# Compact bfloat16 images, borders filled once, and loop constants through DRAM in a fused convolution, state-space and expert kernel

## The chip, the cores and the metric

The kernel runs on one core of one Trainium2 chip. The metric is device time in microseconds. Its median before the change is 2576.19 us over three runs (2576.03 to 2581.16).

## The reference, cut

The input `x` has 128 images of 128 channels and 16 x 16 pixels. Layer 0 is a quantised convolution block; layer 1 treats each image as 256 tokens of 128 channels.

```python
h = _act_quant(_bn(gn(x), gamma1, beta1))        # 4 bits: round(clip(v, 0, 1) * 15) / 15
out = _conv3x3(h, _weight_quant(w1) * pat1)      # pat1: a cross, 5 of 9 taps
out = _act_quant(_bn(out, gamma2, beta2))
out = _conv3x3(out, _weight_quant(w2) * pat2)    # pat2: the diagonals, 5 of 9 taps
x = x + out + gn(x)
t = to_tokens(x)
t = t + mamba(ln(t)) + reverse(mamba(reverse(ln(t))))   # chunks of 64, 4 heads, state 64
t = t + experts(ln(t))                                  # softmax router, best 2 of 8
x = from_tokens(t)
```

`_bn` uses the mean and the variance of the whole batch, so nothing of the first convolution can start before all of `x` has been read, and nothing of the second before the first is done.

## The kernel before

**Loading.** Two images at a time make a tile `xr[i]` of 128 channels x 512 floats (256 KB). There are 64 of them, loaded by SP's queue (L377), and they stay in SBUF through both convolutions. Statistics of each tile run on DVE and ACT as it lands, and become one scale and one bias per image and channel (`sc1`, `bi1`), which hold the group norm, the batch norm and the factor 15 together.

**The two convolutions.** `by_weights` picks one of two programs on a value that the device works out from the weights; here it is the one with five taps and one bfloat16 weight part (`nq` is 1). In the first (`conv1`, from L493), `quantised(i)` brings a tile to the range of the levels: one of its two images by ACT with a Relu (L502), the other mostly by POOL with a scale and a bias (L504) and a second pass that takes the maximum with zero (L506; on DVE for every third tile). `quantise` then writes the levels into one of four padded images `hpads` of 2 x 18 x 18. Before the change these are float32: DVE takes the minimum with 15 and adds the constant `HALF` (L195), which rounds to a whole number n and leaves a float whose lower half is, read as bfloat16, the number 128 + n. `low(hp)` reads only these lower halves, at a step of 4 bytes. `pads` writes the border of all four images on POOL, at the start of each convolution. `conv3x3` (L218) does five matmuls of 128 x 128 weights on 512 pixels, and `offsets` works out what the added 128 contributes, as a constant `less` per channel. ACT takes the result to `o1` (L519), DVE takes its statistics (L520), and SP's queue stores it to DRAM (L522), but for the first five tiles, which are kept (`NKEPT`).

The second (`conv2`, from L546) fetches the `o1` tiles (L558), runs ACT's Relu (L562) and the same `quantise`, convolves, scales the residual `xr` on POOL (L592) or ACT (L590), and adds on DVE (L593). `stored(i)` transposes the sum to tokens (four transposes on PE, L571), scales it on ACT (L573) and stores it to `y_d` (L574). Matmuls of both convolutions have one line, L222, and one name, `cv`.

**The loop.** It works on 64 tiles of 512 tokens. Each part of the work (`part_a` the layer norm and its transposition, `part_c` the step sizes and decays, and so on) is a generator, and a table `T` of hand-written due times per pair of tiles (`PERIOD` 375) gives the order in which their steps are issued; `manual_schedule` keeps that order. `part_a` begins with the load of `yt` from `y_d` (L712), the layer norm (L688 to L706), the transposition `u_ps` (L718) and its copy `uT` (L721). `part_c` begins with the matmul `dt_ps` (L734, L742) and `dtr` on DVE (L748).

Ahead of the loop, `constants` fills three copies of `rows` and `cols` (4 KB of bfloat16 per partition each), which hold the constant part of the segment sums' operands: by ACT (L623), DVE (L624, L628), and POOL, which selects the causal triangle (L635). POOL also zeroes `gts`, `daz` and `lwz` (L646). These tiles take the space of the convolutions, which is released before.

Of the kernel before, what the change touches and what calls it, by code (L numbers as in the profile page):

```python
# [8 lines left out]
F32 = mybir.dt.float32  # L9
BF16 = mybir.dt.bfloat16  # L10
AF = mybir.ActivationFunctionType
ALU = mybir.AluOpType
AX = mybir.AxisListType

P = 128
NT = 256
EPS = 1e-5
MAGIC = 12582912.0
HALF = MAGIC + 0x4300
OFFSET = 128.0  # L20
SCALE = 225.0
NLEV = 15.0
NH = 4
HD = 64
# [3 lines left out]
BIG = 1e38  # L28
LNMIN = 2.0 ** -60
G = 4  # L30
NKEPT = 5


@with_exitstack
def kernel(ctx: ExitStack, tc: tile.TileContext, a: dict):

    nc = tc.nc
    x_d, out_d = a["x"], a["out"]
    B = x_d.shape[0]
    NP = B // 2  # L40
# [16 lines left out]
    cum_d = [dram.tile([G * NH * 4, P], F32, name=f"cum_{i}", tag=f"cum_{i}") for i in range(2)]  # L57


    ident = const.tile([P, P], F32, name="ident")  # L60
    make_identity(nc, ident)
    magic = const.tile([P, 1], F32, name="magic")
    nc.gpsimd.memset(magic, -MAGIC)
    ones = const.tile([P, P], F32, name="ones")
    nc.gpsimd.memset(ones, 1.0)

# [116 lines left out]
        nc.gpsimd.tensor_tensor(w, t, parts[:, :, 1, :], ALU.subtract)  # L183
        nc.scalar.copy(parts[:, :, 2, :], w)

    def low(hp):

        return hp.bitcast(BF16).rearrange("p b h (w two) -> p b h w two", two=2)[:, :, :, :, 0]

    def quantise(q, hp, nq):  # L190

        at = hp[:, :, 1:17, 1:17]
        q4 = q.rearrange("p b (h w) -> p b h w", w=16)
        if nq == 1:
            nc.vector.tensor_scalar(at, q4, NLEV, HALF, ALU.min, ALU.add)  # L195
        else:
            nc.vector.tensor_scalar(q, q, NLEV, MAGIC, ALU.min, ALU.add)
            nc.vector.tensor_scalar(low(hp)[:, :, 1:17, 1:17], q4, MAGIC, None, ALU.subtract)

    def pads(nq):  # L200

        for t in hpads:
            for at in (t[:, :, 0:18:17, :], t[:, :, :, 0:18:17]):
                nc.gpsimd.memset(at, HALF if nq == 1 else 0.0)

    def offsets(pool, psums, wq, taps, nq):

# [10 lines left out]
    def conv3x3(ps, hp, wq, taps, nq):  # L218
        passes = [(tap, q) for tap in taps for q in range(nq)]
        for n, (tap, q) in enumerate(passes):  # L220
            dy, dx = tap // 3, tap % 3
            nc.tensor.matmul(  # L222
                ps, wq[:, tap, q, :], low(hp)[:, :, dy : dy + 16, dx : dx + 16],
                start=(n == 0), stop=(n == len(passes) - 1),
            )

# [34 lines left out]

    ress = ExitStack()
    res = ress.enter_context(tc.tile_pool(name="res", bufs=1))
    wq2 = res.tile([P, 9, 3, P], BF16, name="wq2")

    hpads = [res.tile([P, 2, 18, 18], F32, name=f"hpad{k}") for k in range(4)]
    for t in hpads:
        nc.gpsimd.memset(t, 0.0)
    off = res.tile([P, 2], BF16, name="off")
    nc.gpsimd.memset(off, OFFSET)  # L270
    onec = res.tile([P, P], F32, name="onec")
# [76 lines left out]
    with tc.tile_pool(name="w1p", bufs=1) as w1p:  # L348
# [15 lines left out]
        with tc.tile_pool(name="setup1", bufs=1) as setup, tc.tile_pool(  # L364
# [6 lines left out]
                next(weights)  # L371


            xr = []
            for i in range(NP):
                t = res.tile([P, 2, NT], F32, name=f"xr{i}", tag=f"xr{i}")
                nc.sync.dma_start(t, x_c[:, 2 * i : 2 * i + 2, :])  # L377
                xr.append(t)
            load_weights()
            w2 = w1p.tile([P, 9, P], F32, name="w2", tag="w")  # L380
            nc.sync.dma_start(w2, a["L0_conv_w2"])
# [109 lines left out]
        def conv1(taps, nq):  # L491
            with tc.tile_pool(name="pb", bufs=3) as pb, tc.tile_pool(
                name="psb", bufs=4, space=PSUM  # L493
            ) as psb:
                weights = conv_weights(wq2, how2, w1p, psb, w2, pat2, DIAGONAL, "c2")

                def quantised(i):
                    q = pb.tile([P, 2, NT], F32, name=f"q1_{i}", tag="q", bufs=4)
                    for k in range(2):
                        sc, bi = sc1[:, 2 * i + k : 2 * i + k + 1], bi1[:, 2 * i + k : 2 * i + k + 1]  # L500
                        if k == 0 or i % 10 == 5:
                            nc.scalar.activation(q[:, k, :], xr[i][:, k, :], AF.Relu, bias=bi, scale=sc)  # L502
                        else:
                            nc.gpsimd.tensor_scalar(q[:, k, :], xr[i][:, k, :], sc, bi, ALU.mult, ALU.add)  # L504
                            eng = nc.vector if i % 3 == 0 else nc.gpsimd
                            eng.tensor_scalar(q[:, k, :], q[:, k, :], 0.0, None, ALU.max)  # L506
                    quantise(q, hpads[i % 4], nq)

                pads(nq)
                less = offsets(pb, psb, wq1, taps, nq)  # L510
                for i in range(3):
                    quantised(i)
                for i in range(NP):
                    if i + 3 < NP:
                        quantised(i + 3)
                    ps = psb.tile([P, 2, NT], F32, name=f"cv1_{i}", tag="cv")
                    conv3x3(ps, hpads[i % 4], wq1, taps, nq)
                    o1 = kept[i] if i in kept else pb.tile([P, 2, NT], F32, name=f"o1_{i}", tag="o1")
                    nc.scalar.activation(o1, ps, AF.Identity, bias=less)  # L519
                    behind = nc.vector.bn_stats(o1st[:, i, :], o1.rearrange("p b s -> p (b s)"))  # L520
                    if i not in kept:
                        nc.sync.dma_start(o1_d[i], o1)  # L522
                    if i > 5 and i % 4 == 2:
                        with tc.issue_after(behind.ins):
                            next(weights, None)
                for _ in weights:
                    pass

                mv2 = pb.tile([P, 2], F32, name="mv2", bufs=1)
                nc.vector.bn_aggr(mv2, o1st)  # L530
                rs2 = pb.tile([P, 1], F32, name="rs2", bufs=1)
                nc.gpsimd.tensor_scalar(rs2, mv2[:, 1:2], 1.0 / SCALE**2, EPS, ALU.mult, ALU.add)
                nc.gpsimd.tensor_tensor(rs2, rs2, mhalf[:, 0:1], ALU.pow)
                nc.gpsimd.tensor_scalar(sc2, rs2, gam2, 1.0 / NLEV, ALU.mult, ALU.mult)
                tmp2 = pb.tile([P, 1], F32, name="tmp2", bufs=1)
                nc.gpsimd.tensor_scalar(tmp2, mv2[:, 0:1], sc2, -1.0, ALU.mult, ALU.mult)
                nc.gpsimd.tensor_scalar(bi2, bet2, NLEV, tmp2, ALU.mult, ALU.add)
# [8 lines left out]
    def conv2(taps, nq):  # L546
        with tc.tile_pool(name="pc", bufs=6) as pc, tc.tile_pool(
            name="psc", bufs=4, space=PSUM
        ) as psc, tc.tile_pool(name="psw", bufs=2, space=PSUM) as psw:
            pads(nq)  # L550
            less = offsets(pc, psc, wq2, taps, nq)
            weights = second_weights(pc, psw)
            qs = dict(kept)
# [5 lines left out]

            def quantised(i):  # L560
                q = qs.pop(i)
                nc.scalar.activation(q, q, AF.Relu, bias=bi2, scale=sc2)  # L562
                quantise(q, hpads[i % 4], nq)

            def stored(i):
# [39 lines left out]
    ress.close()  # L605
    kepts.close()

    late = ctx.enter_context(tc.tile_pool(name="late", bufs=1))

# [2 lines left out]
    rows = [late.tile([P, NH, 2, 2, P], BF16, name=f"rows{k}") for k in range(3)]  # L614

    cols = [late.tile([P, 2, 2, 2, 2, P], BF16, name=f"cols{k}") for k in range(3)]
    far = late.tile([HD, 1], BF16, name="far")

    def constants():
        nc.gpsimd.memset(far, -1e30)  # L620
        for k in range(3):
            r, c = rows[k], cols[k]
            nc.scalar.copy(r.rearrange("p h d t l -> p h (d t l)"), heads.unsqueeze(2).to_broadcast([P, NH, 4 * P]))  # L623
            nc.vector.tensor_copy(  # L624
                r[0:HD].rearrange("p h d t (f l) -> p (h d t f) l", l=HD),
                ident[0:HD, 0:HD].unsqueeze(1).to_broadcast([HD, 2 * NH * 2 * 2, HD]),
            )
            nc.vector.tensor_copy(  # L628
                c.rearrange("p m d j f l -> p m (d j f l)"), triple.unsqueeze(2).to_broadcast([P, 2, 8 * P])
            )  # L630
            for d in range(2):
                for half in range(2):
                    sign = 1 - 2 * d
                    for m in range(2):
                        nc.gpsimd.affine_select(  # L635
                            out=c[0:HD, m, d, :, half, :], in_=far.unsqueeze(2).to_broadcast([HD, 2, P]),
                            pattern=[[0, 2], [sign, P]], compare_op=ALU.is_ge, fill=0.0,
                            base=-sign * HD * half - 1, channel_multiplier=-sign,
                        )


    gts = [late.tile([P, P], F32, name=f"gt{k}") for k in range(2)]
    daz = late.tile([P, 2, P], F32, name="daz")
    lwz = late.tile([P, P], F32, name="lwz")
    for t in (*gts, daz, lwz):
        nc.gpsimd.memset(t, 0.0)  # L646
    pr = ctx.enter_context(tc.tile_pool(name="pr", bufs=2))
    sm = ctx.enter_context(tc.tile_pool(name="sm", bufs=2))
    ps_ = ctx.enter_context(tc.tile_pool(name="ps", bufs=1, space=PSUM))
    BANKS = {"x": 2, "y": 2, "o": 4}  # L650
    E0 = 5

# [56 lines left out]
    def part_a(i):  # L709

        yt = yts[i] = pr.tile([P, 4, P], F32, name=f"yt{i}", tag="yt", bufs=6)
        nc.sync.dma_start(yt, y_d[i])  # L712
        yield
        u = pr.tile([P, 4, P], F32, name=f"u{i}", tag="u", bufs=2)
        yield from layernorm(yt, u, f"a{i}")
# [527 lines left out]
            stream = parts[name](i // 2 if len(places) == 1 else i, *which)  # L1243
            steps += [(i // 2 * PERIOD + t, len(steps) + n, stream) for n, t in enumerate(places[i % 2])]
    steps.sort(key=lambda step: step[:2])
    constants()
    with tc.manual_schedule():
        for _, _, stream in steps:
            next(stream)


# [28 lines left out]
```

## Time and profile before

| | |
|---|---|
| median of three runs | 2576.19 us |
| the profiled execution | 2581.9 us, with a span of 2579.9 us |
| busy in the span | PE 2438.1 us (95%), DVE 2260.6 (88%), ACT 2192.9 (85%), POOL 1656.8 (64%) |
| first matmul of the first convolution | 75.28 us |
| first matmul of the second convolution | 176.19 us |
| last sum of the second convolution (L593) ends | 294.47 us |
| first transposition of the loop (`u_ps`) starts | 313.35 us |
| first `dtr` starts | 318.82 us |

The times in the table's lower half are counted from the start of the span. PE is busy in 95% of the span, but that is an average: the first 320 us, before the loop is under way, have other limits, and a change to them is to be read in them. In the lines of the profile, PE is the matmul engine, PEld its weight loads, DVE the vector engine, ACT the scalar engine, POOL the general engine, and SP the engine whose queue issues most DMA transfers. A line of a group or of the timeline names the source line, the operation, its output and inputs, the shape, how often it ran, the busy time, and in brackets or behind a bar the idle time before it and what ended it.

### The profile page before, as it was taken

What the parts mean: (1) busy time and instruction counts of PE and PEld (TensorE: products, weight loads), DVE (VectorE), ACT (ScalarE), POOL (GpSimd) and SP (SyncE); (2) the same over time, 40 slices, a digit from 0 to 9 for tenths busy, and PEclk for the clock granted to TensorE, in tenths of its full rate; (3) what the DMA queues carried; (4) which work ended last, traced back from release to release, by engine and by line L of the source; (5) the groups of instructions that cost most, each with busy time, mean ns of one, the idle gap of its engine ahead of it and who ended that gap; (6) DMA issues with size and microseconds to landing.
All of it is one profiled execution on the core that took longest, in us unless ns stands there. A gap on an engine that the chain in (4) does not pass through costs nothing.

```text
span 2579.9 us, 49413 instructions
## 1 busy us (share of the span) xinstructions
PE 2438.1 (95%) x15940; PEld 1484.6 (58%) x15940; DVE 2260.6 (88%) x6193; ACT 2192.9 (85%) x4482; POOL 1656.8 (64%) x1727
## 2 busy tenths in 40 slices
PE   0879689999999999999999999999999999999997
PEld 0235345666666666666666666666666666666663
DVE  8877589999999999999999999999999999999883
ACT  6777579998988889889888898998888898988881
POOL 1777315666667666666676666666666666666666
PEclk9989889999999999999999999999999999999998
DMA  9458423444444444444434444444444443443343
GB/s 284 147 191 286 166 62 90 123 122 120 127 122 112 130 131 125 124 124 122 121 112 125 129 129 118 120 129 121 120 120 131 131 122 119 127 125 114 108 126 104
DMA packets 303030, 339.03 MB, mean 131 GB/s; under 512 B 56865, under 2 KB 226849, under 8 KB 302753
## 3 DMA queue, kind: packets, MB, share of 16 engines
q1 hardware_dynamic: 302752, 335.68, 43.2%
q8 instruction: 132, 2.16, 0.3%
q14 instruction: 146, 1.19, 0.2%
HBM read 261.41 MB, written 57.41 MB: 124 GB/s over the span
## 4 chain that ended last, share of the span: by engine, by line
PE 88%; DVE 4%; DMA 3%; POOL 2%; ACT 2%; issue 1%; SPq 0%; POOLq 0%; DVEq 0%; ACTq 0%
PE f_ps L1157 17%; PE x_ps L845 13%; PE y_ps L980 9%; PE z_ps L888 9%; PE o_ps L1040 9%; PE sg L933 5%; PE xt_ps L900 4%; PE y_ps L986 4%; PE g_ps L919 4%; PE cv L222 3%; DMA xr<-in_x 2%; PE n_ps L1013 1%; PE u_ps L718 1%; PE u_ps L1062 1%; PE f_ps L1152 1%
## 5 line engine op out<-in xcount | busy, mean ns | idle before, releaser
L1145 POOL TENSOR_TENSOR gb<-gb,u2T 128x512 f32<-128x512 f32 x512 | 641.3, 1277 | 119.5 <-PE y_ps L986 89.9
L863 DVE SCALAR_TENSOR_TENSOR xc<-x_ps,cw,xc 128x510 f32<-128x510 f32 (+2 forms) x768 | 570.6, 743 | 47.0 <-ACT xc L857 37.2
L996 POOL TENSOR_TENSOR yg<-yg,z 128x512 f32<-128x512 f32 x256 | 325.9, 1279 | 354.5 <-DVE yg L992 155.2
L1157 PE MATMUL f_ps<-gb,ew 128*128 128x512 f32 x1024 | 511.6, 603 | 6.1 <-POOL gb L1145 5.9
L845 PE MATMUL x_ps<-uT,wx 128*128 128x512 f32 x768 | 403.6, 608 | 7.6 <-ACT e L673 3.3
L673 ACT ACTIVATE e<-sg 128x512 f32<-128x512 f32 x512 | 299.8, 592 | 49.6 <-PE sg L933 44.4
L673 ACT ACTIVATE e<-e,ends 128x128 f32<-128x128 f32 x1024 | 325.1, 392 | 0.0
L980 PE MATMUL y_ps<-e,xt 128*64 128x256 f32 x2048 | 317.7, 389 | 0.2 <-DVE yg L992 0.2
L961 DVE TENSOR_TENSOR e<-e,g_ps 128x1024 f32<-128x1024 f32 x256 | 311.2, 1216 | 5.9 <-ACT e L673 2.7
L863 DVE SCALAR_TENSOR_TENSOR bc<-x_ps,cw,bc 128x510 f32<-128x510 f32 (+2 forms) x384 | 286.3, 746 | 20.7 <-ACT bc L857 4.9
L1157 PEld LDWEIGHTS f_ps<-gb,ew 128*128 128x128 f32 x1024 | 181.2, 192 | 173.6 <-issue 137.0
L888 PE MATMUL z_ps<-uT,wz 128*128 128x512 f32 x512 | 271.2, 611 | 1.7 <-DVE xc L863 1.1
L857 ACT ACTIVATE xc<-x_ps,cb,cw 128x512 f32<-128x512 f32 x256 | 199.2, 778 | 63.6 <-PE x_ps L845 57.2
L1040 PE MATMUL o_ps<-wo,yg 128*128 128x128 f32 x2048 | 251.3, 276 | 0.2 <-DVE e L966 0.2
L1040 PEld LDWEIGHTS o_ps<-wo,yg 128*128 128x128 f32 x2048 | 240.5, 193 | 11.1 <-DVE g L1117 8.4
L992 DVE SCALAR_TENSOR_TENSOR yg<-xc,dcol,y_ps 128x512 f32<-128x512 f32 x256 | 189.3, 740 | 50.8 <-PE y_ps L986 47.2
L1028 POOL TENSOR_TENSOR rr<-rr,mhalf 128x8 f32<-128x8 f32 x64 | 110.0, 1719 | 161.5 <-DVE g L1119 82.4
L986 PE MATMUL y_ps<-e,xt 128*64 128x128 f32 x2048 | 198.9, 273 | 0.0
L933 PE MATMUL sg<-rows,cols 128*128 128x256 bf16 x1024 | 192.0, 274 | 5.8 <-ACT e L673 2.9
L222 PE MATMUL cv<-hpad,wq 128*128 128x512 bf16 x640 | 179.3, 423 | 18.8 <-DVE hpad L195 9.7
L986 PEld LDWEIGHTS y_ps<-e,xt 128*64 128x64 f32 x2048 | 146.9, 137 | 74.2 <-DVE e L966 0.5
L980 PEld LDWEIGHTS y_ps<-e,xt 128*64 128x64 f32 x2048 | 118.9, 136 | 101.0 <-issue 53.9
(257 smaller groups left out, 4873.0 us busy)
## 6 DMA issues: line engine op xcount, KB each, us to landing
gb<-gd SPq DMA_DIRECT2D x256, 512.0 KB
e<-cum SPq DMA_DIRECT2D x256, 256.0 KB
xr<-in_x SPq DMA_DIRECT2D x64, 256.0 KB
y<-yt SPq DMA_DIRECT2D x64, 256.0 KB
yt<-y SPq DMA_DIRECT2D x64, 256.0 KB
cc<-bc SPq DMA_DIRECT2D x128, 128.0 KB
out<-ob SPq DMA_DIRECT2D x64, 256.0 KB
o<-o SPq DMA_DIRECT2D x59, 256.0 KB
```

The costliest lines, as they stand in the source:

```text
L673: nc.scalar.activation(out, in_, func, **more)
L845: nc.tensor.matmul(ps, wx[d][:, n * P : (n + 1) * P], uTs[i], start=True, stop=True)
L863: nc.vector.scalar_tensor_tensor(acc[:, :, to], raw[:, :, of], cw[:, d, n, 3 - back : 4 - back], acc[:, :, to], ALU.mult, ALU.add,)
L888: nc.tensor.matmul(ps, wz[:, d, n * P : (n + 1) * P], uTs[i], start=True, stop=True)
L933: nc.tensor.matmul(sg[:, :, of], c_[:, k, d, s, half, :], r_[:, :, d, s, of], start=True, stop=True)
L961: nc.vector.tensor_tensor(e0.rearrange("p h t l -> p h (t l)"), e0.rearrange("p h t l -> p h (t l)"), gps[i, d, k][:, 0:NT].unsqueeze(1).t ...
L980: nc.tensor.matmul(y_ps[64 * q : 64 * q + 64, k, :], xt[:, 2 * k + s0, 64 * h : 64 * h + 64], e0[:, h].rearrange("p t l -> p (t l)"), star ...
L986: nc.tensor.matmul(y_ps[64 * q : 64 * q + 64, k, s1 * P : (s1 + 1) * P], xt[:, 2 * k + s1, 64 * h : 64 * h + 64], e1[:, h, :], start=False ...
L996: large(nc.gpsimd.tensor_tensor(yg, yg, zs[i, d][:, n, :], ALU.mult))
L1040: nc.tensor.matmul(o_ps[:, (2 * j + d) * P : (2 * j + d + 1) * P], ygs[i, d, n][:, t * P : (t + 1) * P], wo[d][:, n, :], start=(n == 0), s ...
L1145: large(nc.gpsimd.tensor_tensor(gb[:, e], gb[:, e], u2Ts[i], ALU.mult))
L1157: nc.tensor.matmul(f_ps, ew[:, e, :], gbs[i, e], start=False, stop=(e == NE - 1))
```

## The change

- The padded images become compact bfloat16. All of each image is filled with 128 once, early on; its number is then 128 + n with n in the low byte, so DVE writes only that byte, as uint8 at a step of two bytes, after a minimum with 15 and a maximum with 0.
- With the maximum in that instruction, the Relus become plain scale and bias and the separate maximum passes go. The share of ACT and POOL in the first convolution's scaling is set anew: ACT does 46 of the 128 images, POOL 82 (70 and 58 before).
- Six `o1` tiles are kept in place of five, and `o1` has five buffers in place of three.
- `rows` and `cols` are built once, on POOL in the load stage, and stored to DRAM (512 KB each) by POOL's queue. `constants` is six loads on SP's queue, placed in the loop's order after an early step. DVE, in place of POOL, zeroes `gts`, `daz` and `lwz`.
- The pools of the loop are opened with `reuse_waits="tile"`: a tile in released space waits for the earlier tiles that it overlaps, and not for the whole of the earlier pool. The loads of the first two `yt` tiles go to POOL's queue, and the first two steps of `part_a` are issued ahead of all others.

The order of the loop's instructions on each engine is otherwise the same. On SP's queue the six loads of constants stand behind the last store of `y` and ahead of the third `yt` load. On DVE the four fills and the statistics of the first three `yt` tiles stand ahead of the first `dtr`.

```diff
-NKEPT = 5
+NKEPT = 6
...
     def quantise(q, hp, nq):
...
         if nq == 1:
-            nc.vector.tensor_scalar(at, q4, NLEV, HALF, ALU.min, ALU.add)
+            low = hp.bitcast(mybir.dt.uint8).rearrange("p b h (w two) -> p b h w two", two=2)[:, :, :, :, 0]
+            nc.vector.tensor_scalar(low[:, :, 1:17, 1:17], q4, NLEV, 0.0, ALU.min, ALU.max)
...
-    def pads(nq):
+    def fill(v):
 
         for t in hpads:
-            for at in (t[:, :, 0:18:17, :], t[:, :, :, 0:18:17]):
-                nc.gpsimd.memset(at, HALF if nq == 1 else 0.0)
+            nc.gpsimd.memset(t, v)
...
-                ps, wq[:, tap, q, :], low(hp)[:, :, dy : dy + 16, dx : dx + 16],
+                ps, wq[:, tap, q, :], hp[:, :, dy : dy + 16, dx : dx + 16],
...
-    hpads = [res.tile([P, 2, 18, 18], F32, name=f"hpad{k}") for k in range(4)]
-    for t in hpads:
-        nc.gpsimd.memset(t, 0.0)
+    hpads = [res.tile([P, 2, 18, 18], BF16, name=f"hpad{k}") for k in range(4)]
+    fill(OFFSET)
...
+            r = setup.tile([P, NH, 2, 2, P], BF16, name="r0")
+            c = setup.tile([P, 2, 2, 2, 2, P], BF16, name="c0")
...
+            for h in range(NH):
+                nc.gpsimd.tensor_copy(
+                    r[:, h].rearrange("p d t l -> p (d t l)"), heads[:, h : h + 1].to_broadcast([P, 4 * P])
+                )
...
+            nc.gpsimd.dma_start(rows_d, r)
+            nc.gpsimd.dma_start(cols_d, c)
...
-                        if k == 0 or i % 10 == 5:
-                            nc.scalar.activation(q[:, k, :], xr[i][:, k, :], AF.Relu, bias=bi, scale=sc)
+                        if i < 3 or i % 3 and k == 0:
+                            nc.scalar.activation(q[:, k, :], xr[i][:, k, :], AF.Identity, bias=bi, scale=sc)
                         else:
                             nc.gpsimd.tensor_scalar(q[:, k, :], xr[i][:, k, :], sc, bi, ALU.mult, ALU.add)
-                            eng = nc.vector if i % 3 == 0 else nc.gpsimd
-                            eng.tensor_scalar(q[:, k, :], q[:, k, :], 0.0, None, ALU.max)
                     quantise(q, hpads[i % 4], nq)
 
-                pads(nq)
+                if nq > 1:
+                    fill(0.0)
...
-                    o1 = kept[i] if i in kept else pb.tile([P, 2, NT], F32, name=f"o1_{i}", tag="o1")
+                    o1 = kept[i] if i in kept else pb.tile([P, 2, NT], F32, name=f"o1_{i}", tag="o1", bufs=5)
...
-                nc.scalar.activation(q, q, AF.Relu, bias=bi2, scale=sc2)
+                nc.scalar.activation(q, q, AF.Identity, bias=bi2, scale=sc2)
...
-    late = ctx.enter_context(tc.tile_pool(name="late", bufs=1))
+    late = ctx.enter_context(tc.tile_pool(name="late", bufs=1, reuse_waits="tile"))
...
     def constants():
...
         for k in range(3):
...
+            nc.sync.dma_start(rows[k], rows_d)
+            nc.sync.dma_start(cols[k], cols_d)
...
-    for t in (*gts, daz, lwz):
-        nc.gpsimd.memset(t, 0.0)
...
+    for t in (daz, lwz, *gts):
+        nc.vector.memset(t, 0.0)
...
-        nc.sync.dma_start(yt, y_d[i])
+        (nc.gpsimd if i < 2 else nc.sync).dma_start(yt, y_d[i])
...
-    constants()
     with tc.manual_schedule():
-        for _, _, stream in steps:
-            next(stream)
+        first = [n for n, (t, *_) in enumerate(steps) if t in [places[0] for places in T["a",]]]
+        for n in first:
+            next(steps[n][2])
+        for n, (t, _, stream) in enumerate(steps):
+            if n not in first:
+                next(stream)
+            if t == T["a",][1][1] and t < PERIOD:
+                constants()
```

## The prediction

> **What bounds the kernel now.** I read first the windows by stage (busy microseconds of PE, PEld, DVE, ACT and POOL, then granted PE clock, DMA share, GB/s), because the change touches only what comes before the loop and the entry into it.
>
> ```profile
> 7.00:57.00 50.00, 3.56 (x10) 2.37 (x10) 46.09 (x152) 35.06 (x114) 4.84 (x16) 1.00 1.10 349
> 75.00:168.00 93.00, 85.83 (x327) 31.26 (x327) 81.72 (x165) 79.33 (x135) 77.33 (x95) 1.00 0.48 173
> 176.00:294.00 118.00, 115.14 (x578) 61.93 (x577) 80.11 (x152) 83.82 (x138) 68.41 (x118) 0.98 0.80 263
> 294.00:320.00 26.00, 6.90 (x32) 2.88 (x31) 12.66 (x40) 12.69 (x18) 20.09 (x38) 0.57 0.20 69
> 345.00:2560.00 2215.00, 2193.78 (x14908) 1370.93 (x14907) 2004.25 (x5553) 1954.93 (x4026) 1463.63 (x1388) 1.00 0.41 120
> ```
>
> Loading x fills the DMA engines (349 GB/s). The first convolution has four engines at 77 to 86 of 93 us. The second is PE's, with DMA close behind. The loop from 345 us on is PE's. The reader is to see in row 4 that the hand-over between convolution and loop runs on POOL. The loop's instructions keep their order in the change, so its 2215 us stand.
>
> Next the groups by shape in the first convolution, and the chain of waits in order of time:
>
> ```profile
> L506 POOL TENSOR_SCALAR q<-q 128x256 f32<-128x256 f32 x38 | 38.3, 1008 | 3.3
> L504 POOL TENSOR_SCALAR q<-xr,sc,bi 128x256 f32<-128x256 f32 x56 | 37.7, 677 | 4.5 <-DVE hpad L195 2.8 <-ACT q L502 1.2 <-ACT o L519 0.4
> L195 DVE TENSOR_SCALAR hpad<-q 128x512 f32<-128x512 f32 x64 | 32.0, 513 | 2.1 <-POOL q L506 1.7
> ```
> ```profile
> 162.09 4.28 DMA o<-o
> ...
> 171.94 3.64 issue
> ...
> 212.12 4.73 DMA q<-o
> ...
> 222.87 0.44 PE yt_ps L571 x4
> 223.31 1.28 PE cv L222 x5
> ```
>
> POOL's two passes make its 76 us. A tile of the second convolution takes 1.28 + 0.44 = 1.72 us on PE, and the chain also stands in DMA there. Third, what one matmul of the convolution takes from start to start (weight loads, one per matmul), against the loop's compact bfloat16 matmul of half the width:
>
> ```profile
> 88.23 0.10 PEld L222 LDWEIGHTS <-wq 128*128 128x128 bf16 x1 [0.16 <-issue]
> 88.48 0.10 PEld L222 LDWEIGHTS <-wq 128*128 128x128 bf16 x1 [0.16 <-issue]
> 88.73 0.10 PEld L222 LDWEIGHTS <-wq 128*128 128x128 bf16 x1 [0.15 <-issue]
> ```
> ```profile
> 441.71 0.39 PE L933 MATMUL sg<-rows,cols 128*128 128x256 bf16 x2
> 441.94 1.04 PE L900 MATMUL xt_ps<-ident,xc 128*128 128x128 f32 x8
> ```
>
> The image matmul comes every 0.255 us for 512 columns. Two of 256 columns take 0.23 us here and 0.21 to 0.22 at other places in the same window, so compact data would take about 0.216. Last, the hand-over in the timeline:
>
> ```profile
> 293.71 0.75 DVE L593 SCALAR_TENSOR_TENSOR xr<-cv,less,xr 128x512 f32<-128x512 f32 x1 [0.97 <-PE cv L222]
> 295.35 2.51 POOL L646 MEMSET gt<- 128x128 f32 x2 [50.94 <-PE yt_ps L571]
> 301.62 9.53 POOL L635 TENSOR_SCALAR_AFFINE_SELECT cols<-far 64x256 bf16<-64x256 bf16 x24
> 311.13 1.03 POOL L699 TENSOR_TENSOR rstda<-rstda,mhalf 128x4 f32<-128x4 f32 x1
> 313.35 3.24 PE L718 MATMUL u_ps<-ident,u 128*128 128x128 f32 x8 [18.12 <-ACT u L704]
> 318.82 0.42 DVE L748 TENSOR_TENSOR dtr<-dt_ps,dtb 128x16 f32<-128x16 f32 x4 [4.16 <-PE dt_ps L742]
> ```
>
> POOL had been idle 51 us, then stands 15.8 us in front of the loop's first layer norm.
>
> **The change part by part.** The profiled execution took 2581.9 us (span 2579.9), 5.7 above the median 2576.2. The sum is of differences in it, taken off the median.
>
> *Constants made while x loads.* POOL gets 12 copies of 512 columns (1.2 us each: an estimate from L592's 0.62 us for 256) and 8 selects (0.435 each), 18 us, in a pause that reaches from 9.8 to 27.4 us: hidden. Its two stores, 1.05 MB, are not: DMA is full, 1.05 MB / 349 GB/s = 3.0 us later, and DVE (46 of 50 us busy) can't make up for it. +3 (0 if stores slip into the pause after 57 us, +3.5 with their own start).
>
> *First convolution, 75.3 to 167.9 us.* POOL's 38 and DVE's 19 max passes go; of the affine passes POOL gets 82, ACT 46 instead of 70, so POOL falls to 82 x 0.677 = 56 us, ACT by 24 x 0.54 (ACT's start to start) = 13 to 66, DVE by 7 to 75. Five output buffers in place of three take away the store waits (4.28 us at the end; 4.12 at 87.6). What is late next is PE: 320 x 0.2555 = 81.8 us, or 320 x 0.216 = 69. At the old spacing I take half of the 10 us of PE's stalls: -5. At the new one DVE's 75 us, times the 1.08 by which the stage now exceeds its busiest engine, gives 81: -10 with a little kept back.
>
> *Compact images.* Whether the spacing falls is the open question. Row: 0.255 against 0.216. The difference may come from the 4-byte step between elements or from the breaks between rows of 16, which stay; no row separates them. [...]
>
> *Low bytes by DVE.* L195's best is 0.404 us for 512 elements. The new form writes one byte at a step of two. [...]
>
> *Pads set once.* The second convolution's first matmul waited for POOL's memsets until 176.19, DVE's image being there at 173.2. POOL still spends its 3.64 us of issue, so the first xr is ready about 176.8 and the first transpose starts at 177.7 instead of 180.4: -3. At the first convolution DVE set the start anyway: -0.
>
> *Second convolution, 176.2 to 294.5.* PE 64 x 1.717 = 110 us plus 8.4 of stalls. At the new spacing 64 x (5 x 0.216 + 0.44) = 97; ACT 64 x (0.80 + 0.58) + 16 x 0.59 = 98; DMA 58 loads, 64 stores and a weight, 32.5 MB, at 323 GB/s (304 GB/s were seen at a share of 0.94) = 101. DMA is late next: 101 + 8.4 = 109, so -9. At the old spacing -0; the one transfer less is hidden behind PE.
>
> *Hand-over.* T is the end of L593, 294.47. POOL loses five memsets and 24 selects, ACT 3 and DVE 6 casts. The first two y tiles are now loaded by POOL's queue, right after its last xr pass (51 us early; nothing else queues there), with waits only on early work. DVE does four memsets (1.3 us, from 0.29 us for 128 columns in the load stage), statistics, then POOL and ACT: PE starts at T+5 instead of T+18.9, and by the old distance (5.5 us) dtr could start at T+10.6. But SP's queue puts six constant loads, 3.1 MB or 9.0 us, ahead of the third y tile, whose statistics stand before dtr on DVE: issue from T+2, landing about T+14, dtr at T+15.4 instead of T+24.3. So -9; -14 if the loads don't collide, 0 if they take twice as long.
>
> Sum: +3 - 10 - 9 - 3 - 9 = -28, 2576.2 - 28 = 2548.
>
> **The rivals.**
> [...]
> [...]
> [...]
> 4. The constant loads use up the whole hand-over gain: -19, 2557.
>
> **How the numbers follow.** Forecast 0.50, rival 1 0.28, rival 2 0.10, rival 3 0.05, rival 4 0.07. The predicted time is the first one's, 2548. Its own range is 2538 to 2555; with rivals 1, 2 and 4 the range runs from 2536 to 2566, rival 3 left out. 0.2% is 5 us, about what a measurement of this kernel tells from no change: faster 0.92, same 0.04, slower 0.04.
>
> **What would show it.** [...] The loop's stretch should be as long as before within 3 us; if it moved by more, the reasoning that only the front changes is wrong.

## The result

The changed kernel takes 2561.52 us (median of four runs, 2561.0 to 2563.89); the kernel before took 2578.41 us beside it (four runs, 2576.03 to 2581.16). The ratio is 0.9936, with a 95% interval of 0.9919 to 0.9953: 16.9 us less. The two profiled executions differ by more, 2579.9 - 2559.9 = 20.0 us of span, since that of before (2581.9 us) lay above its other runs. The terms below are differences of these two profiles.

The windows by stage of the changed kernel (stretch, length, busy microseconds of PE, PEld, DVE, ACT and POOL, granted PE clock, DMA share, GB/s):

```profile
7.00:62.00 55.00, 3.56 (x10) 2.37 (x10) 51.13 (x151) 34.73 (x113) 15.55 (x39) 1.00 1.08 345
80.00:163.00 83.00, 78.79 (x324) 31.13 (x324) 75.21 (x145) 65.47 (x109) 55.63 (x81) 1.00 0.52 190
168.60:283.50 114.90, 105.45 (x578) 59.99 (x577) 80.00 (x156) 86.87 (x143) 70.14 (x114) 0.99 0.84 281
283.50:320.00 36.50, 19.87 (x61) 9.58 (x62) 22.75 (x81) 17.20 (x34) 5.88 (x12) 0.65 0.37 130
```

Loading has become longer, and DVE is busy in 51 of its 55 us. In the first convolution POOL fell from 77 to 56 us. PE's column (78.8 of 83 us) is the fullest, DVE's (75.2) the next, and what PE waits for there is almost only DVE's images (total, times, longest):

```profile
PE cv L217 <- DVE hpad L191: 8.4, 5, 5.9
```

The second convolution is 115 us long, but PE's share of it has fallen and no other column has taken its place: DMA is at 0.84. That line is the one to be explained.

| term (us) | before | after | predicted | measured |
|---|---|---|---|---|
| start of the first convolution | 75.28 | 80.30 | +3 | +5.0 |
| its first to its last matmul | 89.2 | 81.6 | -10 | -7.6 |
| from there to the second convolution | 11.7 | 6.8 | -3 | -4.9 |
| second convolution, first matmul to last sum | 118.3 | 114.8 | -9 | -3.5 |
| last sum to the first `dtr` | 24.4 | 14.7 | -9 | -9.7 |
| from there to the end of the span | 2261.1 | 2261.8 | 0 | +0.7 |
| sum | | | -28 | -20.0 |

The second and third rows are cut at the last matmul. The prediction cuts behind it, at the end of the last statistics of the outputs (167.89 us before, 163.34 after). Cut there, the stage goes from 92.6 to 83.0 us (-9.6 for the predicted -10), and what follows from 8.3 to 5.3 (-3.0 for -3).

The matmul spacing and the byte write: six weight loads that follow each other, from the timeline, and groups of the first convolution.

```profile
90.14 0.10 PEld L217 LDWEIGHTS <-wq 128*128 128x128 bf16 x1
90.35 0.10 PEld L217 LDWEIGHTS <-wq 128*128 128x128 bf16 x1
90.60 0.10 PEld L217 LDWEIGHTS <-wq 128*128 128x128 bf16 x1
90.81 0.10 PEld L217 LDWEIGHTS <-wq 128*128 128x128 bf16 x1
91.06 0.10 PEld L217 LDWEIGHTS <-wq 128*128 128x128 bf16 x1
91.30 0.10 PEld L217 LDWEIGHTS <-wq 128*128 128x128 bf16 x1
```
```profile
L522 POOL TENSOR_SCALAR q<-xr,sc,bi 128x256 f32<-128x256 f32 x82 | 54.3, 671 | 23.8 <-DVE hpad L191 11.5 <-issue 5.2 <-ACT q L520 2.7
...
L191 DVE TENSOR_SCALAR hpad<-q 128x512 uint8<-128x512 f32 x64 | 30.9, 498 | 1.6 <-PE cv L217 1.0 <-issue 0.6
```

There is one load per matmul, and the steps from load to load have two lengths. They go with the column at which a tap begins in the padded image. In the medians over all tiles, a tap at column 0 or 2 takes 0.215 to 0.217 us (above, those of the loads at 90.14 and 90.60), and a tap at column 1, which is 2 bytes off a multiple of four, takes 0.242 to 0.245. Before the change, and with the 4-byte step further down, all five taps take 0.250 to 0.261, whatever their column. The cross has three taps at column 1, so the mean is 0.232 us in the first convolution (0.255 before); the diagonals have one, so it is 0.222 in the second. Why column 1 costs more, no run here shows. The byte write takes 498 ns in the mean, 15 less than the float write. POOL, one pass instead of two, now waits for DVE's images.

The load stage on DVE, in the timeline:

```profile
9.91 1.56 DVE L81 TENSOR_SCALAR sums<-sums 128x128 f32<-128x128 f32 x1
...
13.63 4.44 DVE L354 TENSOR_SCALAR grp<-grp 128x128 f32<-128x128 f32 x1
```

Both took about 0.2 us before. POOL's builds of `rows` and `cols` run from 7.8 to 19.5 us, and the second of the two instructions of DVE ends only when POOL pauses to issue its store:

```profile
14.07 1.17 POOL L376 CAST r<-heads 128x512 bf16<-128x512 f32 x2
15.19 1.17 POOL L379 CAST r<-ident 64x512 bf16<-64x512 f32 x2
16.32 1.12 POOL L390 TENSOR_SCALAR_AFFINE_SELECT c<-far 64x256 bf16<-64x256 bf16 x3
17.39 0.60 POOL L386 CAST c<-triple 128x512 bf16<-128x512 f32 x1
17.94 0.77 POOL L395 DMA_DIRECT2D rows_d<-r  x1
```

The second convolution's waits of ACT (total, times, longest), and pieces of the chain of waits there:

```profile
ACT q L582 <- DMA q<-o: 16.2, 18, 1.6
```
```profile
237.86 0.66 issue
238.51 0.59 ACT yt L593
239.12 0.32 SPq L594
239.44 0.05 issue
239.53 4.04 DMA q<-o
```

This reads: ACT finishes a `yt`, SP's queue can then issue its store, and only behind that the next fetch; 4.04 us later its tile is there and ACT goes on. DMA was at 0.84 in this stage, so it was not full all the time.

The hand-over in the timeline:

```profile
285.46 1.05 POOL L700 TENSOR_TENSOR rstda<-rstda,mhalf 128x4 f32<-128x4 f32 x1 [44.54 <-DVE rstda L697]
...
287.71 3.24 PE L719 MATMUL u_ps<-ident,u 128*128 128x128 f32 x8 [3.47 <-ACT u L705]
...
296.78 0.87 DVE L694 BATCH_NORM_STATS2 s6a<-yt 128x6 f32<-128x128 f32 x4 [10.16 <-DMA yt<-y]
...
298.12 0.41 DVE L749 TENSOR_TENSOR dtr<-dt_ps,dtb 128x16 f32<-128x16 f32 x4
```

PE starts the loop 4.2 us behind the last sum. `dtr` stands on DVE behind the third tile's statistics, and these wait 10.16 us for that tile, which lands behind the constants.

### The profile page after: what moved, and what is told of

The parts are those of the page before. It is cut to its first block, busy times and chain, and to the rows that moved or that the text cites. A ratio compares the mean times of both kernels' runs of the same rounds, so it can differ in the third digit from the quotient of the medians.

```text
span 2559.9 us, 49341 instructions
## 1 busy us (share of the span) xinstructions
PE 2420.2 (95%) x15940; PEld 1483.1 (58%) x15940; DVE 2251.0 (88%) x6171; ACT 2174.3 (85%) x4455; POOL 1631.6 (64%) x1692
## 4 chain that ended last, share of the span: by engine, by line
PE 87%; DVE 5%; POOL 2%; ACT 2%; DMA 2%; issue 1%; SPq 0%; DVEq 0%; POOLq 0%; ACTq 0%
PE f_ps L1158 17%; PE x_ps L846 13%; PE y_ps L981 9%; PE z_ps L889 9%; PE o_ps L1041 9%; PE sg L934 5%; PE xt_ps L901 4%; PE y_ps L987 4%; PE g_ps L920 4%; PE cv L217 3%; POOL xr L612 2%; PE n_ps L1014 1%; PE u_ps L1063 1%; PE f_ps L1153 1%; PE u_ps L719 1%
## 5 line engine op out<-in xcount | busy, mean ns | idle before, releaser
L967 DVE TENSOR_TENSOR e<-e,g_ps 128x512 f32<-128x512 f32 x256 | 174.0, 680 | 0.0
```

## The experiments

Twelve kernels, each an edit of the changed kernel. Total times are medians; stages are read in one profile each. The stretch from `dtr` to the end was 2258.0 to 2261.9 us in all of them, so totals of single profiles differ by up to 4 us that no edit accounts for, and stages are the sharper reading. The changed kernel's own runs span 2561.0 to 2563.89 us. The runs of three buffers, copies on ACT, fetch 8, written order with fetch 8, third y and constants in place overlap them, so for these six the stages carry the reading, not the totals.

| kernel | median, us | ratio to before (95%) | first matmul | 1st conv. | gap | 2nd conv. | to `dtr` |
|---|---|---|---|---|---|---|---|
| changed kernel | 2561.52 | 0.9936 (0.9919-0.9953) | 80.3 | 81.6 | 6.8 | 114.8 | 14.7 |
| three `o1` buffers | 2564.64 | 0.9948 (0.9931-0.9965) | 80.3 | 80.5 | 10.3 | 115.3 | 14.7 |
| 4-byte step | 2569.94 | 0.9972 (0.9961-0.9984) | 80.4 | 85.3 | 8.4 | 120.7 | 14.0 |
| copies on ACT | 2557.32 | 0.9917 (0.9899-0.9934) | 76.8 | 82.7 | 6.8 | 115.2 | 14.6 |
| late stores | 2566.24 | 0.9954 (0.9937-0.9971) | 88.0 | 81.1 | 6.8 | 116.3 | 14.6 |
| fetch 8 | 2561.29 | 0.9930 (0.9913-0.9947) | 80.5 | 81.4 | 6.8 | 118.4 | 14.5 |
| written order, fetch 5 | 2572.36 | 0.9977 (0.9966-0.9987) | 80.6 | 80.2 | 6.8 | 129.7 | 14.0 |
| written order, fetch 8 | 2561.18 | 0.9930 (0.9913-0.9946) | 80.6 | 81.2 | 6.8 | 116.1 | 14.5 |
| and stores a tile later | 2552.47 | 0.9903 (0.9886-0.9919) | 80.4 | 80.2 | 6.8 | 106.0 | 14.3 |
| third y on POOL's queue | 2558.16 | 0.9929 (0.9910-0.9947) | 80.5 | 80.9 | 6.8 | 114.7 | 13.3 |
| four early y loads | 2557.66 | 0.9920 (0.9904-0.9937) | 80.6 | 81.4 | 6.8 | 114.4 | 9.7 |
| constants in place | 2564.46 | 0.9944 (0.9928-0.9961) | 75.3 | 81.2 | 6.9 | 114.7 | 24.7 |
| together | 2545.10 | 0.9870 (0.9854-0.9886) | 77.0 | 80.8 | 6.8 | 108.0 | 9.7 |

### What compact images are worth

A kernel with three `o1` buffers again serves as the base, since float images need the space.

```diff
-o1 = kept[i] if i in kept else pb.tile([P, 2, NT], F32, name=f"o1_{i}", tag="o1", bufs=5)
+o1 = kept[i] if i in kept else pb.tile([P, 2, NT], F32, name=f"o1_{i}", tag="o1", bufs=3)
```

> The changed kernel with three o1 buffers again in place of five; nothing else differs. It is also the base for the next run. If the store waits of the first convolution were worth what the prediction gave them (about half of 10 us), the stretch from its first matmul to its last (81.6 us in the changed kernel) grows by 2 to 5 us. If DVE (75 of 83 us busy) bounds it, it grows by less than 1 us. Weight loads stay 0.22 us apart.

The stretch of matmuls did not grow (80.5 us), as was expected if DVE is the bound. The time came back behind it: the last output waits for a store again, as a piece of the chain shows, and the gap grows by 3.5 us.

```profile
159.96 4.24 DMA o<-o
```

So the buffers gain 3.5 us at the end of the stage, or 2.4 if the 1.1 us by which the matmuls' stretch fell is taken off. The expectation, looking for it between the matmuls, missed this.

```diff
-low = hp.bitcast(mybir.dt.uint8).rearrange("p b h (w two) -> p b h w two", two=2)[:, :, :, :, 0]
+low = hp.bitcast(mybir.dt.uint8).rearrange("p b h (w four) -> p b h w four", four=4)[:, :, :, :, 0]
...
-hpads = [res.tile([P, 2, 18, 18], BF16, name=f"hpad{k}") for k in range(4)]
+hpads = [res.tile([P, 2, 18, 18], F32, name=f"hpad{k}") for k in range(4)]
```

> The same with three o1 buffers, and the images laid out at a 4-byte step again: DVE still writes one byte per element, borders are still filled once, PE reads the lower bfloat16 half of every 4 bytes. If the step between elements made the 0.255 us spacing, it comes back (0.222 with compact images), a tile of the second convolution takes PE 5 x 0.255 + 0.44 = 1.72 us again, and against the three-buffer compact run the first convolution grows by 2 to 6 us and the second by about 3 to 4 (from 114.8 to 118), 5 to 10 us in all. If the spacing comes from the breaks between rows or from the border's alignment, it stays at 0.22 and the time within 1 us.

The spacing came back. Weight loads in the timeline of this kernel:

```profile
183.09 0.10 PEld L221 LDWEIGHTS <-wq 128*128 128x128 bf16 x1 [0.15 <-issue]
183.35 0.10 PEld L221 LDWEIGHTS <-wq 128*128 128x128 bf16 x1 [0.16 <-issue]
183.61 0.10 PEld L221 LDWEIGHTS <-wq 128*128 128x128 bf16 x1 [0.16 <-issue]
```

0.255 us in the mean again, with the breaks between rows of 16 the same in both. So the step between elements makes it, and it makes the taps alike. The first convolution grew by 4.8 us and the second by 5.4, the gap shrank by 1.8, and the median rose by 5.3. The 4-byte step also costs the write: durations (least, median, most) of the image write in this kernel, and in the changed one:

```profile
L195 DVE TENSOR_SCALAR hpad<-q x122: 477/499/2644, 79.9 to 287.9; 128x512 uint8<-128x512 f32 x122
```
```profile
L191 DVE TENSOR_SCALAR hpad<-q x122: 407/425/2590, 79.8 to 277.2; 128x512 uint8<-128x512 f32 x122
```

So part of the 4.8 us is DVE's, not PE's; how much was not separated.

### The load stage

```diff
-nc.gpsimd.tensor_copy(   # three places
+nc.scalar.copy(
```

> The changed kernel with the 12 copies that build rows and cols on ACT in place of POOL; the selects and both stores stay where they are. Theory: DVE's two small tensor_scalars in the load stage (sums 1.56 us, grp 4.44 us; 0.21 and 0.22 before the change) stand still while POOL copies, and DVE, which is busy throughout, never makes it up. Then they fall to about 0.2 us, and the first matmul of the convolution comes at 76 to 78.5 us (80.3 in the changed kernel; the stores' 1 MB still makes x land some 3 us late). Rival: the whole 5 us are the stores' traffic; then the first matmul stays at 80 to 80.5 whatever DVE does.

The first matmul came at 76.78, and the stalled instruction in the timeline of this kernel is short again:

```profile
12.66 0.31 DVE L354 TENSOR_SCALAR grp<-grp 128x128 f32<-128x128 f32 x1
```

3.5 of the 5.0 us were DVE standing still beside POOL. (The two instructions stood 5.6 us longer than before; with that gone, DVE is early enough to wait 1.16 us for `x` at 25.4 us.) The remaining 1.5 us were to be moved out of the loads:

```diff
-nc.gpsimd.dma_start(rows_d, r)      # ahead of load_weights()
-nc.gpsimd.dma_start(cols_d, c)
+nc.sync.dma_start(rows_d, r)        # behind all loads
+nc.sync.dma_start(cols_d, c)
```

> The copies on ACT as in the run before, and the two stores of rows and cols on SP's queue behind all loads of x and the weights, where the DMA engines have a pause (9 to 20 GB/s for some 6 us). With the copies on ACT the first matmul came at 76.78 us, 1.5 later than before the change. Theory: the rest is the stores' 1 MB among the loads, so it comes at 75.2 to 75.9 us now and the total falls by another 1 to 1.5 us. Rival: the rest is ACT's own copies, which hold back its share of the statistics; then it stays at 76.5 to 77.

Wrong by 12 us the other way. SP's queue took about half a microsecond for each of the many small weight loads (0.38 to 0.59 us for most) and came to the two stores at 80.9 us only. The first convolution reuses the space from which they read:

```profile
86.46 0.16 DVE L210 TENSOR_SCALAR less<-less_ps 128x1 f32<-128x1 f32 x1 [15.38 <-DMA rows_d<-r]
```

So the pause of the DMA engines wasn't free here: the queue that should use it was busy issuing for most of the time up to 80.9 us. But this trace, with the copies on ACT and no store among the loads, also tells what the 1.5 us are. Its last statistics of `x` on DVE, against those of the run before:

```profile
61.15 0.75 DVE L440 BATCH_NORM_STATS2 bst<-xr 128x6 f32<-128x256 f32 x2
```
```profile
62.93 0.74 DVE L440 BATCH_NORM_STATS2 bst<-xr 128x6 f32<-128x256 f32 x2
```

Without the stores they are 1.8 us earlier, and as early as before the change (60.94). ACT's copies cost nothing there; the stores' traffic is the rest, about half of the 3 us that the prediction gave it.

### The second convolution

```diff
-            for i in range(5):
+            for i in range(8):
                 fetch(i)
...
-                fetch(i + 5)
+                fetch(i + 8)        # and 9 buffers in place of 6
```

> The changed kernel with the o1 tiles of the second convolution fetched 8 tiles ahead in place of 5 (9 buffers in place of 6). Theory: the stage isn't bound by DMA bandwidth but by the 4 us that a fetch takes once it is issued, behind the store of y on SP's queue and so behind ACT's yt. Then ACT's waits for q<-o (16.2 us) fall below 6 us and the stage, from its first matmul to the last sum, goes from 114.8 to 102 to 109 us. Rival (the prediction's, DMA bandwidth): the moved 32 MB need about 101 us plus start and end, so it stays within 2 us of 114.8.

Neither: the stage took 118.4 us, and ACT's waits hardly fell. (This profile was the slowest of four runs; the median, 2561.29 us, is that of the changed kernel.)

```profile
ACT q L582 <- DMA q<-o: 14.4, 15, 3.2
```

The order of the instructions explains it. In the changed kernel's trace, SP's queue mostly issues the fetch of tile i+11 behind the store of tile i, and ACT passes over tile i+9 behind the `yt` of tile i. In this run these are mostly i+14 and i+12. The pass moved forward with the fetch, and the lead of the fetch over its use stayed at two tiles: 3.7 us from issue to pass in the median of the changed kernel, 4.2 here. (The next expectation puts the pass at the fetch's own place, with no lead; the traces don't bear that out.) So the order was fixed:

```diff
+            with tc.manual_schedule():
                 for i in range(NP):
                     ...
-                    with tc.issue_after(behind.ins):
                         next(weights, None)
```

> The changed kernel with the main loop of the second convolution issued in the order in which it is written (fetch 5 tiles ahead as before). In the changed kernel and in the run with 8 tiles the scheduler put ACT's pass over a fetched tile as far ahead of the stores as the fetch itself stands (11 and 14 tiles), so that a fetch is wanted as soon as it is issued. Here a fetch stands 7 tiles ahead of the store beside it and its use 5: a lead of 2 tiles, 3.1 us, against 4 us that a fetch takes. Theory (the lead decides): ACT's waits for q<-o stay at about 1 us per tile at worst and the stage lies between 106 and 116 us. Rival (bandwidth): 112 to 117, as before.

> The same with the fetch 8 tiles ahead in 9 buffers: 10 tiles ahead of the store beside it, its use 5, a lead of 5 tiles or 7.7 us. Theory (the lead decides): ACT's waits for q<-o fall from 16.2 us below 4, PE's 64 tiles of 1.544 us with start and end make 101 to 106 us in place of 114.8, and the total falls by 9 to 13 us. Rival (DMA bandwidth; 32.3 MB at the 300 to 323 GB/s seen in the full slices are 100 to 108 us plus start and end): 109 to 115. Rival (the order as written makes another wait on ACT or DVE): 115 or more.

With fetches 5 ahead the stage grew to 129.7 us, worse than expected. The lead is two tiles, as in the changed kernel, so it can't be what the 15 us are; the written order itself makes other waits, and which of them cost the most was not separated. With 8 ahead, no wait for a fetch is left in ACT's list (all of its lines over 2 us):

```profile
ACT yt L593 <- ACT q L582: 12.1, 28, 0.8
ACT yt L593 <- PE yt_ps L591: 8.7, 13, 2.0
ACT kept L582 <- DVE less L210: 4.7, 1, 4.7
ACT yt L593 <- DMA y<-yt: 3.4, 3, 2.0
```

Yet the stage took 116.1 us, as the third theory had it. PE's timeline shows 1.77 us a tile; the transposes begin only when the matmuls before them have ended, and the next expectation tells the ring of waits behind that:

```profile
221.32 1.27 PE L217 MATMUL cv<-hpad,wq 128*128 128x512 bf16 x5
222.62 0.63 PE L591 MATMUL yt_ps<-ident,xr 128*128 128x128 f32 x4
223.09 1.27 PE L217 MATMUL cv<-hpad,wq 128*128 128x512 bf16 x5
```

```diff
-                    stored(i - 1)
+                    stored(i - 2)
```

> The second convolution in written order with the fetch 8 tiles ahead, and each tile's transposes and y store issued one tile later (tile i-2 beside the convolution of tile i). In the run before, ACT's waits for fetched tiles had gone, but the stage stayed at 116.1: a ring of transposes (0.44), ACT's yt (0.6) and q (0.8), DVE's image write and sum (0.5 + 0.75) and the handings-over between them, some 3.5 us, closed once in two tiles, 1.77 us a tile. Closed once in three tiles it allows 1.17 us. Theory (waits, not bandwidth): PE's 1.544 us a tile decides, the stage takes 100 to 106 us and the total falls by 9 to 14 us against the changed kernel. Rival (DMA bandwidth is the floor after all): 108 to 115.

The stage took 106.0 us, and PE's tile is 1.545 us, with the transposes close behind the matmuls:

```profile
199.79 1.27 PE L217 MATMUL cv<-hpad,wq 128*128 128x512 bf16 x5
200.90 0.60 PE L591 MATMUL yt_ps<-ident,xr 128*128 128x128 f32 x4
201.33 1.27 PE L217 MATMUL cv<-hpad,wq 128*128 128x512 bf16 x5
```

The same 32.0 MB now move at 302 GB/s (281 in the changed kernel), so bandwidth was not what kept the stage at 115. Three edits made this together: the written order, the deeper fetch and the later store. The later store in the scheduler's order, or with fetches 5 ahead, was not run. Bandwidth isn't far off either: 32.0 MB at the 322 GB/s of the changed kernel's fullest slice would be 99 us, as long as PE's 64 x 1.545 = 99.

### The hand-over

```diff
-(nc.gpsimd if i < 2 else nc.sync).dma_start(yt, y_d[i])
+(nc.gpsimd if i < 3 else nc.sync).dma_start(yt, y_d[i])
```

> The changed kernel with the first three y tiles loaded by POOL's queue in place of two, so that the third no longer stands behind the six constant loads on SP's queue. Theory: DVE's wait of 10.2 us for that tile, ahead of the first dtr, goes; dtr then starts 6 to 9 us behind the last sum (14.7 in the changed kernel) and the total falls by 5 to 7 us. Rival: the constants or the step after them are late next (the fourth y tile, or rows and cols for the first segment sums); then dtr comes early but the rest from dtr on grows by as much and the total stays within 1.5 us.

Only 1.4 us came at `dtr` (13.3 in place of 14.7), since the load now stood on POOL behind the layer norm of the first two tiles, and by then the constants were under way:

```profile
288.48 0.63 POOL L713 DMA_DIRECT2D yt<-y  x1 [0.25 <-ACT u L705]
```
```profile
294.95 0.87 DVE L694 BATCH_NORM_STATS2 s6a<-yt 128x6 f32<-128x128 f32 x4 [8.82 <-DMA yt<-y]
```

```diff
-(nc.gpsimd if i < 2 else nc.sync).dma_start(yt, y_d[i])
+(nc.gpsimd if i < 4 else nc.sync).dma_start(yt, y_d[i])
...
-if t in [places[0] for places in T["a",]]]
+if t in [places[0] + k * PERIOD for places in T["a",] for k in range(2)]]
```

> The changed kernel with the first four y tiles loaded by POOL's queue, and the third and fourth loads issued with the first two, right after POOL's last pass over xr, some 44 us ahead of the hand-over (with three on that queue, the third load was issued only at 288.5, behind the layer norm of the first two, and DVE still waited 8.8 us for it). Theory: the wait goes, dtr starts 4 to 9 us behind the last sum (14.7 in the changed kernel), total -5 to -9. Rival: the constants, landing 11 to 13 us behind the last sum, are late next; then the stretch from dtr on grows by as much and the total stays within 1.5 us.

The wait for the tile is gone and `dtr` starts at +9.7, 5.0 us earlier, though a little later than the 4 to 9 expected. What is late next is PE's own `dt_ps`, as before the change:

```profile
286.21 0.86 DVE L694 BATCH_NORM_STATS2 s6a<-yt 128x6 f32<-128x128 f32 x4
...
292.85 0.42 DVE L749 TENSOR_TENSOR dtr<-dt_ps,dtb 128x16 f32<-128x16 f32 x4 [4.16 <-PE dt_ps L743]
```

The stretch from `dtr` on didn't grow (2261.3), so the constants are not late. The median fell by 3.9 us, less than the 5 to 9 expected. One thing more is to be seen in this entry to the loop. In windows of this run the clock granted to PE is 1.00 up to 287 us, and then half of it for a while:

```profile
289.00:303.00 14.00, 11.26 (x45) 6.64 (x45) 7.22 (x32) 7.70 (x17) 2.27 (x4) 0.50 0.42 162
```

It was 0.50 in the changed kernel too (289 to 307 us), and before the change (298 to 330), so `dt_ps`, which is late next, ran at half the clock.

Last, `rows` and `cols` made in place as before the change, everything else as in the changed kernel:

```diff
-            nc.sync.dma_start(rows[k], rows_d)
-            nc.sync.dma_start(cols[k], cols_d)
+            ...                                      # the old body: ACT's copies, DVE's casts, POOL's selects
```

> The changed kernel with rows and cols made in place ahead of the loop again, by ACT, DVE and POOL as before the change, so without the builds, stores and loads of constants; the waits by tile, the early y loads and DVE's memsets stay. The first matmul returns to 75 to 75.6 us (80.3 in the changed kernel). Theory: the selects (10 us of POOL) and casts stand ahead of the layer norm again, u_ps starts 14 to 18 us behind the last sum (4.2) and dtr 20 to 24 (14.7), so the total is 1 to 5 us above the changed kernel's. Rival: by the waits by tile these builds slip in while the convolution still runs (POOL is idle for 45 us); then dtr starts 6 to 12 us behind the last sum and the total is 5 to 13 us below the changed kernel's.

The first matmul is back at 75.3 and `dtr` at +24.7. POOL's timeline, last sum at 278.14:

```profile
280.06 8.01 POOL L628 TENSOR_SCALAR_AFFINE_SELECT cols<-far 64x256 bf16<-64x256 bf16 x8 [48.55 <-DVE cols L621]
...
295.13 1.04 POOL L692 TENSOR_TENSOR rstda<-rstda,mhalf 128x4 f32<-128x4 f32 x1
```

The waits by tile and the early loads give nothing while these selects stand in front of the layer norm. The detour through DRAM is worth 10.0 us here and costs 5.0 in the load stage; in the medians 2.9 us are left of it.

### Together

> Together: copies of rows and cols on ACT, the second convolution in written order with fetches 8 tiles ahead and stores one tile later, and four early y loads. If each part keeps what it is expected to bring (3.5 us in the load stage as measured, 9 to 14 in the second convolution, 5 to 9 at the hand-over) the total is 17 to 26 us below the changed kernel's, 2535 to 2545. If the parts hide one another (the four y loads fall into the second convolution's DMA, the constants are late next) it is 2545 to 2555.

2545.1 us, ratio 0.9870 (0.9854 to 0.9886): 16.4 us below the changed kernel, between the two expectations, and the best of all kernels here. The load stage kept 3.3 us, the hand-over 5.0, and the second convolution 6.8 of 8.8; two more y loads fall into it now, which may be why.

## Why the prediction was right, and where it was wrong

The sign was right, and 2561.5 us lies in the wide range (2536 to 2566). But it is outside the forecast's own range (2538 to 2555), though most of the forecast's mechanisms are the ones that were seen. The wide range holds it only because rivals 1, 2 and 4 were let in, and all three proved false; that the measured time is next to rival 1's 2562 is chance. The gain was 28 us in the sum, 20.0 in the profiles and 17 in the medians. Of the 8 us between sum and profiles, 5.5 are the second convolution and 2.0 the constants.

*Constants made while x loads: the failed assumption.* "18 us, in a pause that reaches from 9.8 to 27.4 us: hidden." POOL's pause was there, but DVE, which had no idle time to give, was held up by what POOL ran in it: two instructions of 0.2 us took 1.56 and 4.44. That is 3.5 us for a part taken as 0. The stores were taken as 3 and cost about 1.5, so two errors in part cancel, and the 5.0 us still lie outside the bounds of 0 to 3.5 that the term was given. DVE's longer instruction stood through eight POOL instructions in a row (14.07 to 17.99 us), until POOL issued its store at 17.94; the shorter one got through at 11.47 while POOL's row went on. Why DVE stands there, no trace shows. That POOL's copies made it stand, the run with copies on ACT does: the longer instruction took 0.31 us in it, and the first matmul came 3.5 us earlier.

*First convolution and the gap behind it.* -13 predicted, -12.5 measured, and by the prediction's own cut each part was right: -9.6 for -10 and -3.0 for -3. DVE has its 75 us, and PE waits for its images, as reasoned. PE's own need was set too low: 320 matmuls at 0.232 us are 74 us, not 69, and so as much as DVE's.

*Compact images.* The sum stands on 0.216, where the only compact bfloat16 row ran; measured 0.216 for taps at an even column and 0.243 at column 1, or 0.232 and 0.222 in the means of the two convolutions; 0.255 in the run with the 4-byte step. In rival 1 (2562 us) the spacing stays at 0.255; no run of compact images shows that, so it is out. A spacing that is alike whatever the tap's column (0.250 to 0.261) is seen at the 4-byte step alone. But compactness brought 5.3 us of median (7.7 by the stages up to `dtr`, a part of it DVE's write), not the 14 between the forecast's 2548 and rival 1.

*Low bytes by DVE.* The forecast's 75 us of DVE keep the image write at its old price, and so it came: 0.407 us at best and 0.425 in the median, for 0.404 and 0.456 before, with 75.2 us of DVE in the stage. Rivals 2 and 3 reckoned with byte writes slower than that (rival 3 with a time above the kernel before). No run shows such a price for a byte write at a step of two, so both are out. At a 4-byte step the write is 0.499 in the median.

*Second convolution: the mis-sized term.* "101 + 8.4 = 109, so -9"; it was 114.8. I had the right neighbour, DMA, by its bandwidth. What the chain already showed in the profile of before (4.73 us of DMA q<-o) was the time of one fetch in a ring with ACT and SP's queue, whose order gives the fetch a lead of two tiles, about as long as it takes (in the changed kernel 3.7 us of lead in the median, and 4.04 us for the fetch in the chain). With the order fixed, the fetch deeper and the store later, the stage takes 106.0 us, 114.8 - 106.0 = 8.8 less, and moves the same bytes. That the 101 us would be the floor of DMA is not refuted by this.

*Hand-over.* -9 predicted, -9.7 measured: `u_ps` at +4.2 for 5, `dtr` at +14.7 for 15.4, and for the reason given, the third y tile behind the constants. Rival 4 is out.

## What to carry to other kernels

Before work is moved into an engine's pause, look at what the neighbouring engine runs then: here a build in POOL's pause came back as a stall of DVE, 3.5 us at the start of the convolution. When a stage has no full column in the windows, look for a ring of waits in the chain; a deeper prefetch brought nothing here while the consumer's place in the issue order moved along with it (118.4 us with fetch 8, for 114.8). And a load that is wanted early has to stand early on its queue: changing the queue alone moved it behind other waits, and brought 1.4 us at `dtr` where the early place brought 5.0.

## What the runs showed of the hardware

A DVE `tensor_scalar` of 128 elements, 0.22 us before the change, stood for 4.44 us while POOL ran casts and selects back to back. DVE's bn_stats beside POOL's casts and selects kept its 0.36 us (three in 1.07 us from 11.39). In the first convolution an image write, 0.425 us in the median, took 2.59 us beside POOL's instruction of 2.54:

```profile
135.37 2.54 POOL L183 TENSOR_TENSOR w<-t_c,wq 128x1152 f32<-128x1152 f32 x1
```
```profile
135.61 2.59 DVE L191 TENSOR_SCALAR hpad<-q 128x512 uint8<-128x512 f32 x1
```

A write of single bytes at a step of two cost no more than one of whole floats (0.407 against 0.404 us at best, 0.425 against 0.456 in the median).

A matmul of 512 columns whose moving operand is compact bfloat16 in rows of 16 came every 0.216 us when the rows begin at a multiple of 4 bytes, and every 0.243 us when they begin 2 bytes off. At a step of 4 bytes it came every 0.255 us.
